# A four-layer graph network on one core: the second stage of edges ends behind node block 82 instead of 78

## The chip, the core and the metric

The kernel runs on one core of a Trainium2 chip. A core has a matrix engine (PE, with its weight loads shown apart as PEld), a vector engine (DVE), an activation engine (ACT), GpSimd (POOL), and a sync engine (SP) that only issues transfers. Each engine has its own instruction queue and works through it in order; they wait for each other by semaphores. Transfers move data between the large memory of the chip and the buffers beside the engines. The metric is the device time of one execution, in microseconds (us).

## The reference

A graph has 12,500 nodes with 32 features and 400,000 edges. `src` is random; `dst` is sorted, and low nodes have more edges than high ones (the share of the edges that goes to the first n nodes is the root of n/12500). Four layers follow each other. Each adds its result to x and normalises each row.

```python
edge_index = jnp.stack([src, dst])
x = _layernorm(x + _L0_gnn_ref(x, src, dst, ...))        # attention: softmax over the edges of a node
x = _layernorm(x + _L1_gnn_ref(x, edge_index, 3))        # three rounds: mean of the neighbours
x = _layernorm(x + _L2_gnn_ref(x, edge_index, edge_attr_32, ...))   # an MLP on each edge, maximum per node
x = _layernorm(x + _L3_gnn_ref(x, edge_index))           # three rounds: sum of the neighbours, scaled
...
# L2, on each edge
e_feat = jnp.concatenate([x[rol], x[col], edge_attr], axis=-1)
h = jax.nn.relu(e_feat @ W1 + b1)
v = h @ W2 + b2
x_cand = jax.ops.segment_max(v, col, num_segments=num_nodes)
return jnp.maximum(x_cand, x[:, -v.shape[-1]:])
# L3, one of three rounds
msgs = norm[:, None] * x[src]
x = jax.ops.segment_sum(msgs, dst, num_segments=n)
```

## The kernel before

Nodes are cut into H = 98 blocks of 128. A round of L1 or L3, a sum over the neighbours of every node, is done as a dense product: the kernel first builds the count matrix A (how many edges go from node s to node t, one byte each, 12,544 x 12,544, kept in the large memory), and then multiplies it with x. x stands in `x3` as three bf16 parts side by side (96 columns), so that nothing is lost.

`Rounds.product` is one such round. It takes the targets in 25 chunks c of 512 nodes (four blocks, the last chunk two) and, for each target block, one matmul per source block h: a 128 x 128 piece of A is the weight, the 96 columns of x3[h] stream past it (L382, 96 columns). It takes the source blocks from `lo` on; with lo = 0 that is 98 for each of 98 target blocks. Before the chunks comes a small extra product on `Ax`, for edges beyond what the build of A has room for in a chunk (c = -1, 392 matmuls of 128 columns, L377, then z at L310); its result is added to the first 14 chunks (L272). Loads of A go through SP (L354 where lo is above 0, two chunks of A in a buffer, L363 otherwise), into three buffers. Finished chunks are summed on DVE (L278).

The edge layer L2 (`edge_layer`) works on the edges themselves. A first part of them, 308 columns of 128 edges, is handled by `heavy` beside the rest. The other 2,817 columns are walked in stages. A stage s ends behind node block HS[s], and with the blocks a cut in the columns is fixed, with a margin of five deviations (`cuts`). A stage is cut into batches of up to T = 48 columns, and a batch into groups of four columns. For one group, POOL gathers four times the source rows from `table` (`ef<-table,ids`, L111), PE transposes them (pT, L1751), DVE copies (eT, L1753), PE and ACT run the MLP (`hidden`, L1782 to L1787, and `outer`, L1800). POOL may run up to AHEAD = 4 groups ahead, since a group's indices (`ids`, L1729) are copied behind an earlier group's eT. A batch also loads keep, attr and begin through SP (L1603, L1608, L1611), spreads the rows of the target nodes by 32 scans on DVE (L1628), takes running maxima by 32 more (L1637), and writes `scan` (L1640). At most two batches have an ef buffer; attr and begin have one.

The scans are emitted six to a group (`steps(6)`); those that a batch still lacks when it begins are emitted there at once.

When the last batch of a stage has its maxima, `end(s)` joins the partitions (a gather and a scatter, fx, on POOL), eight groups of delay among it, and `done(s)` gathers the maxima of the stage's node blocks from `scan` (`ends<-scan,end_i`, one gather for each block, in sets of G = 8), and finishes the layer on these blocks: layer norm, and x3 of L3's first round (`split`, its last step L258). `end` and `done` go on one step for each group (`tick`); behind the last stage they run through.

The stages are there for this: as soon as a stage's blocks have their x3, L3's first round can take their share while POOL still gathers edges. `round_part(s)` does that. It turns the product around: x3[h] is the weight (96 columns), and 512 targets of A stream past (L1366, 512 columns), for all 25 chunks and the blocks hs[s] to hs[s+1]. Each chunk's sum is copied (ys, L1373), turned by eight small matmuls (z, L284) and added to `part` (L1351). A chunk's blocks are loaded in pieces of up to HP = 16 blocks through SP (L1361), into three buffers. The steps are handed out by `fill`, called twice for a group, 40 steps on the first call of a part and eight on each later one; a step is one matmul. What is left when the edges are through is emitted behind the loop.

```python
hs = (0,) + HS + (H,)                       # L213
...
size = -(-(hi - lo) // -(-(hi - lo) // HP)) # L1342, in round_part
...
k = 8 if fillers[0] in begun else 40        # L1384, in fill
...
R.product(x3, post3, (), 0 if r else HS[-1])  # L1532: L3's rounds
```

So L3's first round consists of two parts of fill, blocks 0 to 51 and 52 to 77, and of a short product behind the edge layer, over the remaining 20 blocks (lo = HS[-1]). Memory for the product's buffers is taken over from the edge layer's.

The code gives the order only as a priority: a planner arranges each engine's queue at compile time from the order of the text, the dependences and its own costs, so an instruction may move ahead of an earlier one that it thinks is not ready. Tables for the edges (`edge_tables`) are prepared in pieces of at most 261 columns during L1.

With HS = (52, 78) the cuts are 308, 2292, 2804 and 3125: stages of 1984, 512 and 321 columns, in 42, 11 and 7 batches and 496, 128 and 81 groups. Stage 1's last batch has 32 columns.

Of the kernel before, what the change touches and what calls it, by code (L numbers as in the profile page):

```python
# [57 lines left out]

SPAN = 60.0
ONE = 512.0  # L60
HS = (52, 78)
EARLY = 2
CX = 14
HC = 308
# [56 lines left out]
def dense_path(ctx, tc, bad_i, x, src, dst, edge_attr, w1T, w1_b, w2, w2T, w2_b, aT,  # L121
# [90 lines left out]

    hs = (0,) + HS + (H,)  # L213
    cuts = [HC]
    for h in HS:
        f = (h * P / N) ** 0.5
        cuts.append(-(-int(E * f + 5 * (E * f * (1 - f)) ** 0.5) // P // 4) * 4)
    cuts.append(C)
    heads = []
    for s in range(len(HS) + 1):  # L220
        heads.append((
# [259 lines left out]
    def edge_tables(st):  # L481
# [25 lines left out]
        todo = []  # L507
        for s in range(len(HS) + 1):
            Cs = cuts[s + 1] - cuts[s]
# [166 lines left out]
    with ExitStack() as build:  # L676
# [164 lines left out]
        def slots():  # L841
# [31 lines left out]
            yield  # L873
            for s, h in enumerate(HS):
                w = slice(h % 4 * (P // W), h % 4 * (P // W) + 1)
# [313 lines left out]
    with ExitStack() as st:  # L1189
# [3 lines left out]
        with tc.tile_pool(name="seg", bufs=1) as seg, \  # L1193
# [18 lines left out]
            nc.vector.tensor_scalar(tot, tot, -1.0, 0.0, op0=OP.add, op1=OP.max)  # L1212
            for s in range(len(HS) + 1):
                sl = slice(hs[s], hs[s + 1])
# [1254 lines left out]
```

## Time and profile before

| what | us |
|---|---|
| median of 18 runs | 7686.87 (7679.53 to 7704.0) |
| the profiled execution | 7693.49 |
| its span, first to last instruction | 7691.6 |
| first matmul of the first fill, L1366 | at 5599.4 |
| last gather of an edge column | at 6549.2 |
| last matmul group of the second fill done | at 6594.2 |
| x3 of the last blocks written, short product goes on | at 6631 |
| first matmul of L3's second round | at 6751.9 |

The granted clock of PE was 0.832 on average. A page of the profile gives, for each engine, busy time in 40 slices of the span (tenths; 9 is 90% or more) and the granted clock likewise. A table by stage gives for chosen stretches the busy time of each engine with the number of instructions, then the granted clock, the share of time in which the transfer engines were busy, and GB/s. A line of the order of time gives the start, the length, the engine, the source line, the operation with the names of its output and inputs, and in brackets how long the engine was idle before it and what ended that. Where equal instructions follow each other closely they stand in one line with their number.

### The profile page before, as it was taken

The numbers are of one execution on the slowest core, as the hardware profiler recorded it, in microseconds if no ns is written. First come the engines' busy times: TensorE is split into PE (matmuls) and PEld (weight loads), VectorE is DVE, ScalarE is ACT, GpSimd is POOL, SyncE is SP. The second block draws the span as 40 slices with busy tenths as digits, with TensorE's granted clock in tenths as the row PEclk, the third lists the DMA queues.
The fourth block names the chain that finished last, engine by engine and source line by source line (L and its number), as shares of the span: only waits on it lengthen the run. The fifth ranks groups of instructions, "written<-read, shape, count | busy, mean of one in ns | idle before, by whom it ended". The sixth has DMA issues, their size and how long they took to land. (4 is left out here: it accounts for less than half of the span.)

```text
span 7691.6 us, 194318 instructions
## 1 busy us (share of the span) xinstructions
PE 6654.0 (87%) x84402; PEld 5288.6 (69%) x84402; DVE 3923.3 (51%) x10962; ACT 1635.5 (21%) x3386; POOL 3579.3 (47%) x3459
## 2 busy tenths in 40 slices
PE   6788999899999987888888888778669979899998
PEld 4678899889999984555555555434335645799998
DVE  6989899561554555555555555433344333411121
ACT  1334688200000002222222222211112212100000
POOL 1002501000655727777777777777777777100000
PEclk7879999999999996677777777555559968999999
DMA  2128544899999982222222222221227836799998
GB/s 51 65 109 323 196 202 198 301 334 361 361 373 354 362 323 78 62 55 55 59 55 63 55 55 59 51 60 46 52 74 225 250 87 185 247 352 366 356 355 311
DMA packets 574338, 1447.42 MB, mean 188 GB/s; under 512 B 108023, under 2 KB 269407, under 8 KB 560031
## 3 DMA queue, kind: packets, MB, share of 16 engines
q1 hardware_dynamic: 432816, 1347.10, 47.9%
q0 software_dynamic: 109792, 66.25, 5.1%
q10 hardware_dynamic: 30864, 21.54, 1.0%
q8 instruction: 664, 10.88, 0.6%
q14 instruction: 202, 1.65, 0.1%
HBM read 1155.33 MB, written 279.27 MB: 187 GB/s over the span
## 5 line engine op out<-in xcount | busy, mean ns | idle before, releaser
L111 POOL DMA_INDIRECT ef<-table,ids x2817 | 2677.0, 950 | 881.7 <-issue 654.5
L382 PE MATMUL y<-x,a 128*128 128x96 bf16 x49980 | 2217.1, 206 | 98.3 <-issue 97.3
L382 PEld LDWEIGHTS <-a 128*128 128x128 fp8e4 x49980 | 2156.0, 98 | 130.1 <-issue 128.0
L1751 PE MATMUL pT<-ident,ef 128*96 128x128 f32 x2817 | 770.8, 356 | 569.2 <-DMA ef<-table,ids 552.9
L1751 PEld LDWEIGHTS pT<-ident,ef 128*96 128x96 f32 x2817 | 398.5, 162 | 1026.3 <-DMA ef<-table,ids 681.5
L1753 DVE COPY eT<-pT 96x512 f32<-96x512 f32 x705 | 476.7, 676 | 1047.1 <-PE pT L1751 1046.6
L1019 PE MATMUL pa<-oh,ol 128*128 128x196 bf16 x4928 | 734.7, 273 | 121.2 <-DVE oh L1009 75.7
L1800 PEld LDWEIGHTS pv<-mw,hT 128*128 128x128 f32 x3208 | 598.1, 260 | 269.1 <-issue 94.0
L1025 ACT ACTIVATE at<-pa 128x784 uint16<-128x784 f32 x816 | 646.9, 824 | 506.2 <-PE pa L1019 477.5
L1800 PE MATMUL pv<-mw,hT 128*128 128x64 f32 x3208 | 679.5, 349 | 22.5 <-ACT hT L1787 15.2
L1787 ACT ACTIVATE hT<-ph,mb 128x256 f32<-128x256 f32 x802 | 380.5, 474 | 1332.2 <-PE ph L1784 1304.7
L1019 PEld LDWEIGHTS <-ol 128*128 128x128 bf16 x4928 | 558.9, 150 | 136.3 <-issue 74.8
L1055 PE MATMUL y<-x,at 128*128 128x102 bf16 x9604 | 641.6, 210 | 10.2 <-DVE x L258 6.0
L1782 PE MATMUL ph<-eT,mw 96*64 96x256 f32 x1410 | 627.1, 538 | 11.8 <-DVE eT L1753 10.3
L1784 PE MATMUL ph<-eT,mw 96*64 96x256 f32 x1408 | 629.4, 540 | 0.0
L278 DVE TENSOR_REDUCE v<-y 128x128 f32<-128x384 f32 (+2 forms) x152 | 83.4, 548 | 1067.3 <-PE y L272 582.0
L1009 DVE TENSOR_TENSOR oh<-bins_h,pl 128x1568 bf16<-128x1568 bf16 x616 | 594.6, 965 | 0.0
L111 POOL DMA_INDIRECT g<-code_d,ws_i x25 | 216.0, 8639 | 810.2 <-DVE ki L793 591.1
L116 POOL DMA_INDIRECT sorted_d<-hrow,pos x308 | 409.8, 1331 | 381.2 <-DVE v L1249 190.6
L1055 PEld LDWEIGHTS <-at 128*128 128x128 fp8e4 x9604 | 558.4, 98 | 23.6 <-issue 11.6
L1366 PE MATMUL y<-a,x 128*96 128x512 fp8e4 (+1 forms) x1950 | 492.4, 389 | 2.4 <-DVE x L258 1.5
L1004 DVE TENSOR_TENSOR ol<-la,lb 128x1024 bf16<-128x1024 bf16 x616 | 419.4, 683 | 69.5 <-PE pa L1019 69.1
(409 smaller groups left out, 6816.3 us busy)
## 6 DMA issues: line engine op xcount, KB each, us to landing
a<-A SPq DMA_DIRECT2D x245, 3136.0 KB
A<-at SPq DMA_DIRECT2D x98, 1568.0 KB
a<-A SPq DMA_DIRECT2D x144, 832.0 KB
ef<-table,ids POOLq DMA_INDIRECT x2817
starts_d<-rows SPq DMA_DIRECT2D x44, 1024.0 KB
attr<-in_edge_attr SPq DMA_DIRECT2D x57, 768.0 KB
begin<-starts_d SPq DMA_DIRECT2D x57, 768.0 KB
scan<-o SPq DMA_DIRECT2D x57, 768.0 KB
```

What stands on the lines that cost most here:

```text
L111: return nc.gpsimd.indirect_dma_start(out=o, out_offset=None, in_=tab, in_offset=IndirectOffsetOnAxis(ap=idx, axis=0))
L382: nc.tensor.matmul(y[:, q, :], block(h, q - q0), x3[:, h, :3 * F], start=(q + h == first), stop=(c >= CX and q == nq - 1 and h == H - 1))
L1009: nc.vector.tensor_tensor(oh, bins_h[:, None].to_broadcast([P, 4, HJ, 2]), pairs(pl[:, t, 0, half * 64 + w0:half * 64 + w0 + 8])[:, :, Non ...
L1019: nc.tensor.matmul(pa[:, 2 * b + i, :HJ], ols[t][:, :, :, 4 * u + 2 * b + i].rearrange("p a b -> p (a b)"), ohs[t][:, 2 * u + b, :, i], st ...
L1025: nc.scalar.activation(at[:, qd, :, off:off + 8].rearrange("p h (w j) -> p h w j", w=4), pa[:, :, :HJ].rearrange("p w (h j) -> p h w j", h ...
L1055: nc.tensor.matmul(y[0][:, q, :], at[:, q - 2 * half, h, :], x3[:, h, :3 * F0], start=(q + h == 0), stop=(not EARLY <= c < CX and last and ...
L1366: nc.tensor.matmul(y[:3 * D, :nq * Q], x3[:, h, :3 * D], a[:, :nq, h - h0, :], start=(h == lo), stop=(h == hi - 1))
L1751: nc.tensor.transpose(pT[:3 * D, j, :], B.ef[:, t + j, :], ident)
L1753: behind = nc.vector.tensor_copy(eT[:, :k], pT[:3 * D, :k])
L1782: nc.tensor.matmul(ph[:HID, :ka], mw1, eT[:, :ka], start=True, stop=True)
L1784: nc.tensor.matmul(ph[HID:2 * HID, :k - 2], mw1, eT[:, 2:k], start=True, stop=True)
L1800: nc.tensor.matmul(pv[:, j].rearrange("p h d -> p (h d)"), hT[:, j, :], mw2, start=True, stop=True)
```

## The change

One constant is changed. The second stage ends behind block 82. The cuts become 308, 2292, 2872 and 3125: stages of 1984, 580 and 253 columns, in 42, 13 and 6 batches and 496, 145 and 64 groups; stage 1's last batch has four columns, a single group. The second part of the fill has 30 blocks (52 to 81) in two pieces of 15 instead of two of 13, `done(1)` has 30 blocks and `done(2)` 16, and the short product starts at lo = 82, with 16 source blocks. Edge tables are prepared in 12 pieces as before, three of up to 194 columns for stage 1 and one of 253 for stage 2 (before: two of 256, and 161 and 160).

```diff
@@ -58,7 +58,7 @@
 
 SPAN = 60.0
 ONE = 512.0
-HS = (52, 78)
+HS = (52, 82)
 EARLY = 2
 CX = 14
 HC = 308
```

## The prediction

> **What bounds the kernel now.** I first read the page's slices of the span, to find which engine is full where. Slices are 192 us long, so the edge layer's end (6100 to 6600 us) is slices 32 to 35.
>
> ```profile
> PE   6788999899999987888888888778669979899998
> POOL 1002501000655727777777777777777777100000
> PEclk7879999999999996677777777555559968999999
> ```
>
> POOL is level at 7 through the edge layer, while PE and its clock go up and down. The table by stage, with stages cut where the second fill starts and ends, says why.
>
> ```profile
> core 0: us, PE busy (x) PEld busy (x) DVE busy (x) ACT busy (x) POOL busy (x), PEclk, DMA share, GB/s
> 6195.00:6395.00 200.00, 140.99 (x452) 68.93 (x452) 76.91 (x298) 32.40 (x85) 151.55 (x160) 0.56 0.23 59
> 6395.00:6570.00 175.00, 175.00 (x1038) 111.45 (x1037) 60.13 (x230) 35.75 (x85) 110.03 (x117) 1.00 0.71 216
> 6594.00:6631.00 37.00, 9.39 (x96) 8.73 (x95) 14.42 (x49) 2.84 (x9) 19.21 (x20) 0.62 0.69 254
> 6651.00:6740.00 89.00, 87.20 (x1989) 86.08 (x1987) 53.62 (x167) 13.11 (x44) 0.00 (x0) 1.00 0.84 305
> ```
>
> From 6195 to 6395 there is nothing to fill with; POOL starts a gather every 1.25 us (160 in 200 us) and sets the pace. From 6395 PE is full: edges and fill compete, and POOL falls behind its pace. From 6594 to 6631 PE has 9 us of work in 37. Then the short product is PE's. The same table for the fill's matmuls alone (L1366) gives their number:
>
> ```profile
> core 0: us, PE busy (x) PEld busy (x), PEclk, DMA share, GB/s
> 6395.00:6570.00 175.00, 121.91 (x503) 58.65 (x504) 1.00 0.71 216
> 6570.00:6595.00 25.00, 18.54 (x92) 10.37 (x90) 1.00 0.56 164
> ```
>
> The order of time shows the seam (start, length, work, and the idle time before it with its cause):
>
> ```profile
> 6383.00 1.09 PE L1366 MATMUL y<-a,x 128*96 128x512 fp8e4 x2 [0.17 <-DVE x L258]
> ...
> 6549.18 0.95 POOL L111 DMA_INDIRECT ef<-table,ids  x1 [0.34 <-DVE ids L1729]
> 6570.25 0.27 PE L1751 MATMUL pT<-ident,ef 128*96 128x128 f32 x1
> 6577.89 7.09 PE L1366 MATMUL y<-a,x 128*96 128x512 fp8e4 x32
> 6588.28 0.95 POOL L111 DMA_INDIRECT fx<-scan,fix  x1 [38.16 <-DMA a<-A]
> 6593.53 0.63 PE L284 MATMUL z<-S,ys 96*128 96x32 f32 x4 [0.51 <-ACT ys L1373]
> 6604.39 5.83 PE L377 MATMUL y<-a,x 128*96 128x128 fp8e4 x56 [10.22 <-issue]
> 6618.10 0.94 POOL L111 DMA_INDIRECT ends<-scan,end_i  x1 [0.30 <-issue]
> 6717.78 21.93 PE L382 MATMUL y<-x,a 128*128 128x96 bf16 x512 [0.33 <-issue]
> 6751.87 23.68 PE L377 MATMUL y<-a,x 128*96 128x128 fp8e4 x392 [3.26 <-DMA a<-Ax]
> ```
>
> The second fill starts as the last x3 block of stage 1 is written (6383), the last edge column is transposed at 6570, the fill ends at 6594.2, and the gathers of the last 20 node blocks end at 6619. Only when their x3 is written (6631) does the short product go on. So fill and edges end almost together, and the tail of `done(2)` is what PE waits for.
>
> **The change, part by part.**
>
> *Where the second fill starts.* Groups of four columns are the clock of the emission. Stages have 496, 128 and 81 groups before and 496, 145 and 64 after. Counting yields: `end(1)` begins 14 groups after stage 1's end (17 after the change, because its last batch is one group long), `done(1)` another 14 later, and `round_part(1)` is appended 19 later (21 with 30 blocks). That is group 671 of 705 before, 693 after. The first call takes 40 steps, each later one 8, two calls a group: 40+8+33·16 = 576 of 25·26 = 650 matmuls are emitted inside the loop before; 40+8+11·16 = 224 of 25·30 = 750 after. Left behind the loop: 74 before, 526 after. The trace fits the first count: 92 matmuls from 6570 on, 74 plus one group's 16.
>
> *Time of that start.* The 22 groups in between are paced by POOL: 22·4 gathers and 4 more end gathers in `done(1)`, at 1.25 us, 115 us. PE becomes full at 6395+115 = 6510. Lower bound 100 (three groups of the count are scan pacing that could shrink), upper 135 (below, the short batch).
>
> *The full stretch.* Before it lasts 6395 to 6594.2, 199.2 us. Taken out: 22 groups of edge work. In the 175 us row, 503 fill matmuls at 0.216 (32 in 7.09 us, less the last one's tail) are 108.6 us and 160 z matmuls (20 chunks at 0.82) 16.4; the other 50 us are 31 groups, 1.6 each: -35.2. Put in: 100 matmuls at 0.216, +21.6. So 185.6 us, and the fill ends at 6695.6. Check from the other side: the last transposes come some 8 us earlier than before, at 6562, since POOL is less held back; 542 matmuls, 18 z and the edges' rest of 4.5 us follow, 117+15+4.5, giving 6698.
>
> *Loads of the fill on SP.* Still 50 issues, but 15 blocks each instead of 13, 6.5 MB more. A chunk of 1.97 MB is used up in 30·0.216+0.82 = 7.3 us, 270 GB/s. The trace sustained 246 GB/s from 5800 to 6180 beside edge traffic and 305 in the short product, so I take no wait; at 246 it would be 0.7 us for each of 17.5 chunks, +12, and at the 216 GB/s of the row above 1.8, +32. Queued behind these loads on SP is only the last `scan` write, and the x3 that hangs on it has some 70 us to spare.
>
> *The tail of stage 2.* 16 gathers, not 20: -5 us on POOL, and one `finish` less. It now ends near 6615, under the fill, so it costs and gains nothing. If the fill were short again it would be worth 5 us.
>
> *The short product (lo 82).* 98·4 = 392 matmuls of 96 columns fewer, at 0.0425 (512 in 21.93): -16.7 us. Its loads fall by the same 6.5 MB; they are hidden by PE before (87 of 89 us) and stay so. Between the fill's end and the next round's first matmul lie 157.7 us before (6594.2 to 6751.9). After: 10.2 waiting for `Ax` (no longer hidden, but there already), 392 L377 at 60 to 66 ns, 25; 97.8 (6650.8 to 6748.6) less 16.7, 81.1; the next `Ax` wait, 3.3, grows by 1.7 since the last two and a half chunks cover less of a load: 5. Sum 121.3, a gain of 36.4. Of this, some 20 us are simply the PE wait that the longer fill has moved into.
>
> *One batch more.* 61 instead of 60: two keeps, attr, begin and a scan write on SP, and 64 scans of 0.2 to 0.3 us on DVE, which is busy 77 of 200 us: free. But stage 1's last batch is a single group, so 26 of the next batch's 32 scans are forced at its start, and its gathers must wait for the PE to finish the batch before the short one. No row has this; the same place before has 8 forced scans and no POOL gap. From nothing to 20 us; I take 0, as POOL runs several groups ahead and PE has 59 us of slack in that stretch. Preparation of the edge tables keeps 12 chunks and every element: nothing.
>
> *Sum.* 6695.6 - 6594.2 - 36.4 = +65 us. On the profiled execution, 7693.49 (span 7691.6), that is 7758; it stood 6.6 above the median, so for the median 7686.87 I forecast 7752.
>
> **A page against the trace.** PE streams 216 ns for each 512-column matmul in the row of 32 and 42.5 ns for each 96-column one in the row of 512. The Trainium skill, "TensorE: Matmul & The Clock Gate", section "Back-to-back issue gap", gives about 131 ns at 512 columns and 81 at 128 for a stream of weight loads and matmuls. By the page the 100 added matmuls would cost 13 us and the 392 removed save 32, an estimate of +41 instead of +65: it speaks for the change, and the rows contradict it.
>
> **The rivals.**
>
> Faster: the planner draws the fill forward so that it still ends under the tail. PE has 59 idle us from 6195 to 6395 (clock 0.56), which speaks for it; but x3 blocks 52 up exist only when `done(1)` has written them, and before the change the fill started within a microsecond of the last. The point is a fill's end of 6631: 65 us, 300 matmuls, would have to find room earlier. If all did, the time falls by 16.7+5-1.7 = 20, to 7667.
>
> Same: half of that room is found, or the 22 groups shrink to about 10; the fill ends within 15 us of 6631. Near 7687.
>
> Slower still: the long pure fill outruns its three load buffers, +12 to +32, so 7764 to 7784. If its waits also let the clock drop to the 0.5 of the unfilled stretches, 526 matmuls at twice 0.216 add 114: 7866.
>
> That the change does nothing is excluded: cuts, groups and blocks all move.
>
> **How the numbers follow.** As worked 0.73 (own range 7735 to 7775, from the bounds on the start, -15 and +20); loads bind 0.15; clock drops 0.03; same 0.05; faster 0.04. Changes of 0.2%, 15 us, are about what a measurement tells here. Slower 0.91, same 0.05, faster 0.04. The range 7718 to 7788 holds the first two cases and leaves out about 0.12 and their edges.
>
> **What would show it.** Right: the fill's matmuls run without edge transposes beside them for over 100 us, ending near 6695; the last end gather lies well before; PE is full from about 6510; the short product has 1568 L382 matmuls in some 81 us; the rest keeps its lengths. Wrong: fill matmuls starting before 6480, their pitch off 0.216, gaps in them released by DMA, or POOL idle at the third stage's start.

## The result and the profile after

The changed kernel takes 7768.23 us (median of 7 runs, 7758.21 to 7782.81) against 7687.17 for the kernel before beside it: a ratio of 1.0105, with a 95% interval from 1.0095 to 1.0115. It is 81 us slower; 65 were forecast, a time of 7752. The profiled execution of it took 7764.42, with a span of 7762.6.

The slices of the page, in order PE, POOL and the granted clock of PE:

```profile
PE   6788999999999988888888888678679978899998
...
POOL 1003401001566637777777777777777775000000
PEclk7889999999999986776777777555579958999999
```

POOL's row is as level as before. Slices of 194 us are too coarse for the rest: where the edge layer ends, slice 33 has a tenth of the clock less (5 instead of 6) and slice 34 a tenth of PE (8 instead of 9). The table by stage, cut where the same stages now lie:

```profile
core 0: us, PE busy (x) PEld busy (x) DVE busy (x) ACT busy (x) POOL busy (x), PEclk, DMA share, GB/s
6179.00:6380.00 201.00, 145.02 (x448) 70.44 (x449) 84.42 (x363) 34.82 (x87) 152.14 (x161) 0.51 0.24 62
6495.00:6549.00 54.00, 52.11 (x301) 32.14 (x300) 21.52 (x88) 9.84 (x24) 31.62 (x34) 1.00 0.73 221
6549.00:6703.00 154.00, 136.72 (x712) 86.19 (x710) 24.13 (x94) 14.52 (x31) 17.37 (x18) 0.93 0.70 219
6736.00:6818.00 82.00, 79.41 (x1811) 78.67 (x1808) 55.23 (x176) 13.71 (x46) 0.00 (x0) 1.00 0.82 290
```

The stretch with edges alone is still paced by POOL (161 gathers in 201 us), PE and edges compete for only 54 us where it was 175, and then comes what was hardly there before: 154 us in which the edges are through and PE works on the fill. In that row the clock is 0.93 and PE is busy for 136.72 of 154 us. The order of time on PE shows where the rest is (start, length, work, and the idle time before it with its cause):

```profile
6548.93 0.27 PE L1751 MATMUL pT<-ident,ef 128*96 128x128 f32 x1
...
6577.18 6.66 PE L1366 MATMUL y<-a,x 128*96 128x512 fp8e4 x30
6584.48 6.65 PE L1366 MATMUL y<-a,x 128*96 128x512 fp8e4 x30
...
6607.44 1.91 PE L284 MATMUL z<-S,ys 96*128 96x32 f32 x8 [16.31 <-ACT ys L1373]
...
6609.17 9.28 PE L1366 MATMUL y<-a,x 128*96 128x512 fp8e4 x30
...
6619.10 6.66 PE L1366 MATMUL y<-a,x 128*96 128x512 fp8e4 x30
...
6702.12 0.63 PE L284 MATMUL z<-S,ys 96*128 96x32 f32 x4 [0.51 <-ACT ys L1373]
```

A chunk of the pure fill takes 7.3 us, 30 matmuls between two z in 6.66 us and the z, from the last transposes at 6549 to the end at 6702.75. But once PE stands for 16.31 us, because z waits for the copy `ys`, and the 30 matmuls behind the hole run at a lower clock, 9.28 us instead of 6.66. ACT's own order says why the copy is late:

```profile
6582.41 0.58 ACT L1373 COPY ys<-y 96x512 f32<-96x512 f32 x1 [6.72 <-PE y L1366]
6603.54 0.21 ACT L243 ACTIVATE ln_s<-ln_s 128x8 f32<-128x8 f32 x1 [20.55 <-DVE ln_s L242]
...
6606.50 0.41 ACT L257 CAST x<-rest 128x256 bf16<-128x256 f32 x1 [0.72 <-DVE rest L256]
6606.81 0.57 ACT L1373 COPY ys<-y 96x512 f32<-96x512 f32 x1
```

L243 belongs to the layer norm of `done(2)`, and L254 and L257 behind it to the writing of x3. L243 waits for DVE, and DVE waits twice for the end gathers of the last 16 blocks, which come in two sets of eight:

```profile
6595.58 0.42 DVE L1309 TENSOR_TENSOR ends<-ends,rest 128x256 f32<-128x256 f32 x1 [17.92 <-DMA ends<-scan,end_i]
...
6603.00 0.42 DVE L1309 TENSOR_TENSOR ends<-ends,rest 128x256 f32<-128x256 f32 x1 [2.98 <-DMA ends<-scan,end_i]
```

The chunk that is to be copied was through at about 6589.7 (24 of the 30 matmuls of the line at 6584.48 belong to it, the last six to the next one; the copy before, at 6582.41, came at the same point of the line at 6577.18). But the copy stands behind L243, L254 and L257 in ACT's queue, and runs 17 us late. Loads are not the cause: no wait of PE in these 154 us is for one, and SP's queue waits for PE to free the buffers (total, times, longest):

```profile
SPq L1361 <- PE y L1366: 122.1, 33, 22.6
```

To hold the two executions against each other I count from the last edge gather of the first stage, which the change doesn't touch (5377.2 before, 5365.8 after). The 11 us between these two are no more than lies between two executions of one kernel: the changed kernel's second trace, on another chip (below), has 5352.0.

| term | before | after | difference | forecast |
|---|---|---|---|---|
| that gather to PE full with the second fill (its 60th matmul) | 1019.4 | 1129.6 | +110.2 | +115 |
| PE full to the fill's end | 197.6 | 207.3 | +9.7 | -13.6 |
| fill's end to L3's second round | 157.7 | 120.1 | -37.6 | -36.4 |
| sum | 1374.7 | 1457.0 | +82.3 | +65 |

From the second round to the end both take 939.7 or 939.8 us. The sum is 17 us over the forecast; the second term alone is 23 over it, and the other two take 6 back.

### The profile page after: what moved, and what is told of

The parts are those of the page before. It is cut to its first block, busy times and chain, and to the rows that moved or that the text cites. A ratio compares the mean times of both kernels' runs of the same rounds, so it can differ in the third digit from the quotient of the medians.

```text
span 7762.6 us, 193783 instructions
## 1 busy us (share of the span) xinstructions
PE 6694.0 (86%) x84110; PEld 5293.6 (68%) x84110; DVE 3925.4 (51%) x11010; ACT 1635.0 (21%) x3385; POOL 3577.1 (46%) x3459
## 5 line engine op out<-in xcount | busy, mean ns | idle before, releaser
L1751 PE MATMUL pT<-ident,ef 128*96 128x128 f32 x2817 | 790.9, 360 | 599.3 <-DMA ef<-table,ids 580.5
L1366 PE MATMUL y<-a,x 128*96 128x512 fp8e4 (+1 forms) x2050 | 508.9, 389 | 1.1 <-DMA a<-A 0.7
```

The costliest lines, as they stand in the source:

```text
L1366: nc.tensor.matmul(y[:3 * D, :nq * Q], x3[:, h, :3 * D], a[:, :nq, h - h0, :], start=(h == lo), stop=(h == hi - 1))
L1751: nc.tensor.transpose(pT[:3 * D, j, :], B.ef[:, t + j, :], ident)
```

## Experiments

My theory was the forecast's with the hole added: the fill starts some 110 us late because the work that releases it goes by groups from a later stage end, what then lies behind the edge loop goes at PE's pace, the short product gives some 37 back, and ACT's queue adds some 20. The rivals: that the four more source blocks cost, with their loads; that the hole is harmless; that the one-group batch stalls the gathers; and that fewer blocks are better all along.

The chips differ. The first four runs were on one that takes 9021.67 us for the kernel before (median of 14 runs); the others were on chips that take 7676.01 (21 runs) and 7687.95 (19 runs). Each run is held against the kernel before on its own chip.

### The two halves of the change

The cut of the edges and the list of blocks come from the same constant; here they are given apart.

```diff
+CUTS = (52, 82)        # edges only: HS stays (52, 78); blocks only: the two exchanged
-    for h in HS:
+    for h in CUTS:
         f = (h * P / N) ** 0.5
...
-            for s, h in enumerate(HS):
+            for s, h in enumerate(CUTS):
```

> Half of the change alone: the edges of stage 2 are cut where the change cuts them (for node block 82), but only blocks up to 78 are made out of that stage, and the fill and the product behind the edge layer stay as before (12 chunk rows of the fill, 20 source blocks behind it). Theory (the fill is made after the stage's last gathers, which the longer stage puts 15 to 20 groups of 6 us later, and what then lies behind the edge loop runs at TensorE's pace; the scalar queue's stalled layer norm adds one hole of about 16 us with a slow chunk behind it, if it falls into the fill): fill start +95 us, fill shorter from full issue to its end by some 32 us, so the fill ends 62 us later, or 82 with the hole; the product behind it has 20 blocks, but its gathered rows wait less, which gives some 20 back. Against before: +42 us without the hole, +62 with it. Rival (the four more source blocks of the fill, their loads and matmuls, are what costs): within 15 us of before.

> The other half: the edge stages stay cut for node block 78, but blocks up to 82 are made out of stage 2 and go into the fill, and 16 source blocks are left behind it. (It leaves out: the maxima of blocks 79 to 81 are gathered before their last edges are through, so a few of their edges don't count.) Theory (late start of the fill): the fill starts within 15 us of before, has 50 more matmuls per pass behind the loop, ends some 34 us later, and the short product gives 36 back: -3 to +17 us against before, the upper end if the hole on TensorE is still there. Rival (more blocks in the fill and their loads are the cost): most of the 81 us, +50 or more.

> The edges' cut for block 82 with the blocks of 78, again, on another chip. Theory (the later end of the stage costs, not the four more blocks): fill start some 100 us later than before, some 410 matmuls behind the loop, the hole of the scalar queue in it, the product with 20 blocks: +50 to +65 us against before. Rival (the blocks cost): within 15 us of before.

Edges alone: 1.0082 (1.0054 to 1.0110), +74 us on the slow chip, 12 more than expected there, and 1.0074 (1.0057 to 1.0091), +56.5 us, on the other, as expected. There the fill's first matmul comes 97 us later than before and its 60th 101, counted from the first stage's last gather, with 410 matmuls behind the last transposes. Blocks alone, in a kernel that leaves out a few edges: 1.0017 (1.0001 to 1.0033), +16 us. So the later stage end is what costs, and the four blocks nearly pay for themselves. The hole is there in the cut-only run too. On the faster chip the profile puts it down to a step of the same layer norm on DVE; but the copy that z reads ended on ACT at 6617.61, 0.05 us before z began, and it stood there directly behind the same L243, L254 and L257 (one line further down in this kernel). PE's line, then ACT's:

```profile
6617.66 1.92 PE L285 MATMUL z<-S,ys 96*128 96x32 f32 x8 [20.17 <-DVE ln_s L238]
```

```profile
6617.03 0.58 ACT L1374 COPY ys<-y 96x512 f32<-96x512 f32 x1
```

With blocks alone a wait of 17.4 us for `ys` was left behind the last transposes.

### The hole in ACT's queue

The layer norms of the last blocks are put behind the fill:

```diff
+            if s == len(HS):
+                while fillers:
+                    fill(0)
+                with tc.issue_after(last[0].ins), tc.issue_after(last[1].ins):
+                    for t in todo:
+                        for _ in finish(*t):
+                            pass
+                return
```

(`last` holds the latest `ys` copy and the latest addition to `part`.)

> The changed kernel, with the last blocks' layer norm and x (the tail of stage 2) put on the scalar and vector queues behind the last copy and the last addition of the fill, so that no copy of the fill stands behind a wait for the end gathers. Theory (the scalar queue's order makes the 16 us hole and the slow chunk behind it): no wait of TensorE over 2 us within the fill, the fill ends some 20 us earlier, and the time is 15 to 20 us under the changed kernel's, +61 to +66 us against before; if the tail then ends too late for the next layer, up to 10 of that are lost again at the first product. Rival (the hole is covered, or TensorE waits for something else there): within 4 us of the changed kernel, +77 to +85.

> The changed kernel itself, on the chip of the runs beside it, so that these can be held against it. +81 us against before on a chip that takes 7687 us for before; on a chip that is slowed to some 9022 us, where a group of the edge loop takes 7.9 us in place of 6.2, the fill's start is moved by 20 to 22 such groups and the change costs more, +95 to +115 us.

> The same kernel as e3_tail_order, now beside the changed kernel on the same chip. Theory (the scalar queue's order makes the hole, and the hole costs its length): 15 to 20 us under the changed kernel. Rival (the slow granted clock would have come anyway, or the delayed tail of stage 2 takes the gain back at the next layer's first product): within 5 us of the changed kernel, although the hole is gone.

The first of these runs showed no wait of PE over 2 us behind the last transposes (ahead of them, beside the edges, one of 10.5 us for `ys`), but the changed kernel wasn't beside it, so its 1.0100 (1.0072 to 1.0128), +93 us on the slow chip, tells nothing of the hole's price. Beside each other on a third chip: the changed kernel 7752.25 us, 1.0102 (1.0083 to 1.0120), +76 us; with the tail behind the fill 7739.17, 1.0079 (1.0063 to 1.0096), +63 us. The medians differ by 13, under the 15 to 20 expected, and the intervals overlap. The two profiled executions as wholes are no help either, 7746.41 and 7746.98: the reordered one comes 15.3 us later to the last gather of the first stage, long before the part that the edit concerns, which is as much as between two executions of one kernel. The traces of the stretch itself are sharper. The fill from the last transposes to its end, in the changed kernel and then in the reordered one:

```profile
core 0: us, PE busy (x) PEld busy (x) DVE busy (x) ACT busy (x) POOL busy (x), PEclk, DMA share, GB/s
6536.00:6690.00 154.00, 136.31 (x712) 85.96 (x709) 24.23 (x94) 14.52 (x31) 17.29 (x18) 0.93 0.69 219
```

```profile
6553.00:6687.00 134.00, 132.93 (x712) 84.43 (x709) 13.23 (x62) 12.56 (x25) 17.05 (x18) 1.00 0.78 251
```

The same 712 instructions take 134 us instead of 154, at a clock of 1.00 and 251 GB/s. The waits of PE in these two stretches:

```profile
PE z L284 <- ACT ys L1373: 16.7, 2, 16.2
```

```profile
PE z L284 <- ACT ys L1383: 0.5, 1, 0.5
```

From the last transposes to the fill's end it is 153.3 against 133.8 us, 19.5 less: 16.2 are the hole, 3.3 the slow chunk behind it. Nothing of it is lost later, since from the fill's end to the second round it is 120.0 in both. Counted as in the table, the reordered kernel's terms are +111.0, -8.6 and -37.7: +64.7. So that the wait on ACT's queue makes the hole is shown; its price is 19.5 us in the traces and 13 in the medians.

### An earlier start of the fill

Even batches in the second stage (g groups of four columns in nb batches, in place of full batches and a rest of one group):

```diff
+            g, t0 = -(-Cs // 4), 0
+            for j in range(nb):
+                n = min(4 * (g // nb + (j < g % nb)), Cs - t0)
+                plan.append((s, t0, n))
+                t0 += n
```

> The changed kernel, with the 332 column tiles of stage 2 in batches of nearly even size in place of full ones and a last batch of one group. Theory (the fill's start is counted in groups from the end of the stage, and the three groups' time of a short batch goes through the count): the fill is made at group 687 in place of 693, starts some 35 us earlier, and the time is 25 to 30 us under the changed kernel's, about +50 against before. Rival 1 (the short batch itself stalls the gather queue): a gap goes from GpSimd and TensorE at the start of stage 3, and more than 30 us are saved. Rival 2 (the batches' size is without effect): +77 to +85 us against before.

This gave 1.0059 (1.0036 to 1.0081), +55 us, on the slow chip: 37 us under the reordered kernel, the only one with the changed cuts and blocks beside it, although the hole is still there (15.9 us). 446 matmuls are left behind the last transposes instead of 542, exactly six groups of 16 fewer, so the count holds. The fill's first matmul comes 51 us earlier than in that run; 38 of them lie behind the end of the second stage, six groups of 6.3 us, and 13 ahead of it, which the count doesn't explain, so on this chip the first rival isn't excluded. On the changed kernel's own chip there is next to nothing of it: POOL stands for 3.22 us behind the one-group batch, where it stood 1.77 at the same place before (6099.14), and then goes on as before, 161 gathers in 201 us:

```profile
6179.08 0.95 POOL L111 DMA_INDIRECT ef<-table,ids  x1 [3.22 <-ACT part L1353]
```

Then the waiting work is taken twice per group in the third stage:

```diff
-            steps(6)
-            tick()
+            for _ in range(2 if B.s == 2 else 1):
+                steps(6)
+                tick()
```

> The changed kernel, with the steps of the waiting work taken twice per edge group in the groups of stage 3, so that the end gathers of stage 2, which release the fill, come after half as many groups. Theory (the fill's late start is the cost): the fill is made at group 667 in place of 693, starts within 15 us of where it does before, ends some 80 to 95 us earlier than in the changed kernel, and the time is -18 to +5 us against before (up to +15 with the hole on TensorE). Rival 1 (the start was not what cost; four more blocks are): +60 to +80 against before. Rival 2 (the edge loop pays for the work that is pushed into fewer groups): the last gather of the edge layer comes more than 15 us later, and +20 to +50.

> Both together: twice the steps per group in stage 3, and the tail of stage 2 behind the fill on the scalar and vector queues. Theory: fill at group 667, no hole on TensorE, -20 to 0 us against before, 0 to 20 under the run with twice the steps alone. Rival (the tail of stage 2, delayed behind the fill, ends last): 5 to 20 us over the run with twice the steps alone.

With the steps doubled, block 82 takes 7672.80 us, 0.9993 (0.9982 to 1.0004): all of the 76 us are gone, and the edit changes only how soon the waiting work, the scans with it, is taken. The fill's first matmul comes 74 us earlier than in the changed kernel (21 later than before; I had said within 15) and its 60th 126 us earlier (17 earlier than before), 126 matmuls are left behind the last transposes instead of 542, and the fill ends 108 us earlier (80 to 95 were expected), 20 of them the hole, which is gone because the end gathers now come back after the fill. The last edge gather comes 8 us later than in the changed kernel, under the 15 of the second rival.

Both edits together: 7661.92 us, 0.9979 (0.9970 to 0.9988), 14 us or 0.2% under the kernel before and the fastest kernel of this study on its chip. But the reorder has no part in that which the trace shows: there was no hole left for it to remove. With the steps doubled alone as with both, PE's waits for `ys` in the fill are one of 0.5 us. In both traces the second round starts 1365 us after the first stage's last gather. The 11 us between their medians are unexplained, and their intervals overlap.

### The neighbours: 80, 74, and an earlier fill at 78

```diff
-HS = (52, 78)
+HS = (52, 80)        # and (52, 74); the third keeps 78 and takes the steps twice
```

> Half of the step: stage 2 ends behind node block 80, so 18 source blocks are left for the product. Theory (the fill's late start against the wait for the tail of stage 2, some 20 us, that the longer fill first has to use up): the fill is made at group 683 in place of 671 (before) and 693 (block 82), starts 60 to 65 us later than before, leaves some 320 matmuls behind the loop, and the time is +25 to +45 us against before. Rival (the cost is in proportion to the blocks added, as that of a loop with four more blocks would be): just half of the change's +76 to +81, and no more wait left at 78 blocks to be used up, so that 74 blocks would gain another 76.

> The same step the other way: stage 2 ends behind node block 74, 24 source blocks are left. Theory (before the change the product waits for the tail of stage 2, not for the fill): the fill is over before the last edges, the first product matmul of the next layer that has to wait for the tail comes within 5 us of where it comes before, and the product is 4 blocks, some 15 us, longer: +10 to +20 us against before. Rival (fewer blocks are better all along): -40 to -80.

> The kernel before, with the steps of the waiting work taken twice per edge group in stage 3: the fill comes earlier, at group 648 in place of 671. Theory (before the change the fill's end isn't what the product waits for): the fill ends inside the edge loop, the tail of stage 2 and all behind it stay, within 8 us of before, and so over the run with block 82 and twice the steps by the four blocks of the product, 10 to 15 us less what that run's fill still costs. Rival (an earlier fill is a gain by itself, whatever the blocks): -15 us or more against before.

Block 80: 7723.23 us, 1.0045 (1.0028 to 1.0061), +35 us, as expected, with 332 matmuls behind the last transposes and a hole of 15.7 us; the fill's first matmul comes 47 us later than before and its 60th 57, a little under the 60 to 65 expected. Block 74: 7682.53 us, 0.9991 (0.9981 to 1.0001), -5 us, no gain or a small one where I expected a loss of 10 to 20. So the times stand at about -5, 0, +35 and +76 to +81 for 74, 78, 80 and 82: flat on one side of the kernel before and steep on the other. No proportion fits that.

What I missed at 74 is not the product. From PE's last wait for a block of the tail (it ends at 6604.00 at 74 and at 6631.18 before) to the second round it takes 134.2 us instead of 120.7: +13.5, near the 15 forecast. But that wait ends 17 us earlier, counted from the first stage's last gather, where I had said within 5. First POOL's order of time, then PE's, at 74:

```profile
6530.44 0.95 POOL L111 DMA_INDIRECT ef<-table,ids  x1 [0.30 <-issue]
6549.96 0.94 POOL L111 DMA_INDIRECT fx<-scan,fix  x1 [18.57 <-DMA scan<-o]
```

```profile
6600.27 1.09 PE L377 MATMUL y<-a,x 128*96 128x128 fp8e4 x8 [10.34 <-DVE x L258]
...
6604.00 6.19 PE L377 MATMUL y<-a,x 128*96 128x128 fp8e4 x72 [1.36 <-DVE x L258]
```

From the last edge gather to the join `fx` it is 19.5 us here and was 39.1 before (6549.18 to 6588.28), where the last groups' transposes and MLP stood among fill matmuls on PE: the last transpose came 21 us after the last gather before, and comes 4 us after it here. So the fill that ran until 6594 before was not free: beside the last edges it delayed the tail that PE then waited for. The run with 78 and doubled steps says the same: its fill is over 68 us before the last gather is issued, and `fx` comes 19.1 us after that gather. In POOL's order of time:

```profile
6554.17 0.94 POOL L111 DMA_INDIRECT ef<-table,ids  x1 [0.30 <-issue]
6573.26 0.94 POOL L111 DMA_INDIRECT fx<-scan,fix  x1 [18.14 <-issue]
```

Of these 20 us only some 5 are left where PE's last wait for the tail ends, since the last edge gather itself comes 9.5 us later than before and the tail behind `fx` takes longer. The run takes 7676.92 us, 0.9984 (0.9974 to 0.9993), -11 us; I had expected no more than 8 either way, and the rival 15 or more. It is on a par with block 82 and doubled steps (0.9993 and 0.9979 on their chip): once the fill is early enough, four blocks more or less in it are not to be told apart. What the shorter product saves at 82, 11.8 us by the same count (106.4 against the 118.2 of this run), the later tail takes back.

## Why the prediction was right, and where it was off

*Where the second fill starts.* The count was right to the matmul: 526 steps behind the loop and one group's 16 were forecast, 542 matmuls follow the last transposes. The even batches, with 96 fewer, confirm it. The time read from the trace was not the start: at 6383 only the last of four sets of x3 blocks was written, and from 6299.9 on, behind the first set, 59 matmuls of the fill had trickled through. So "nothing to fill with" until 6395 and a start "within a microsecond of the last" block were misread, and the sign "fill matmuls starting before 6480" came true without meaning anything: after the change the first is at 6384.9, and again 59 come before PE is full at 6495.5.

*Time of that start.* +115 forecast, +110 measured to the 60th matmul, where PE is full. That it is the cause was shown by the doubled steps, which take this delay away (and with it the hole) and leave cuts and blocks as they are, and by the two halves.

*The full stretch.* This is the mis-sized term: -13.6 forecast, +9.7 measured. Some 19 of the 23 us are the hole and the slow chunk behind it; with these removed the term is -8.6. The 5 us that remain cancel with the 4 of its start and the 1 of its product: the reordered kernel's sum is +64.7 against the +65 of the working. Its other parts held: 6.66 us for 30 matmuls (216 ns each, with the last one's tail), and the last transposes 10 us earlier (forecast: some 8).

*Loads of the fill on SP.* Right, no wait of PE for a load; without the hole the loads went at 251 GB/s.

*The tail of stage 2.* This is the step that failed: "ends near 6615, under the fill, so it costs and gains nothing". It named as cover the fill's length and the 70 us that its x3 has to spare. Both were there: the end gathers were back by 6603, and the last x3 was written at 6612.5. Yet it cost 19.5 us. But the tail's layer norm and the fill's copies share ACT and DVE, and each queue is worked through in order, so a wait that nobody needed to end soon stopped a copy that PE needed at once. The change adds no wait, so I didn't ask who is queued behind one; but an old wait had moved among new neighbours: before, the same layer norm came behind the fill's last copies. The Trainium skill, "TensorE: Matmul & The Clock Gate", section "Architectural detail: the array is 16× 32×32, not 1× 128×128", calls ACT's and DVE's queues strictly first in, first out; the copy at 6606.81, whose input was ready at about 6589.7, agrees.

*The short product.* -36.4 forecast, -37.6 measured, and right in its parts. The runs at 74 and with doubled steps put the four blocks at 11.8 to 13.5 us, where the working had 16.7; the rest was, as the working said, PE's former wait for the tail.

*One batch more.* Nearly nothing, as taken: POOL's wait behind the batch is 1.5 us longer than before. Its three groups were in the count of the start.

*The rivals.* The planner did not draw the fill forward. Loads did not bind. The clock did drop, but for one chunk: 2.62 us on its 30 matmuls and 0.93 on the z before them (1.91 instead of 0.98). Together these are 3.55 us. The same page, section "What's actually happening", has the clock at half after at least one idle window of some 3.4 us and back to full after at least one busy one; with one busy window the hole would have cost 1.7 us behind it, with two 3.4, both estimates, and the rows agree with two.

*The range.* 7768 lies in it, but partly by luck: the room above 7752 was given to a later start and to loads that bind, and neither came.

## What to carry to other kernels

A piece of work that is moved into a stretch shares every engine's queue with what was already there: besides what it costs and what covers it, ask for each in-order queue which of the waiting instructions now stand ahead of work that the bound engine needs. When the start of filling work is counted in steps of another loop, a later release costs one for one what no longer fits beside that loop; releasing it sooner (here, two steps per group) took back all of it, where even batches took back a part. And before a tuned size is moved, look which side of it is flat: in these runs, filling work that ended with the work it fills delayed that by some 20 us, while filling work that ended later added all of what was left of it.

## What was not expected of the hardware

One chip ran its kernels some 17% slower (9021.67 against 7676.01 us for the kernel before). In the same stretch of time, inside the first stage of the edge layer, the blocks-only kernel there and then the kernel before where it was profiled:

```profile
core 0: us, PE busy (x) PEld busy (x) DVE busy (x) ACT busy (x) POOL busy (x), PEclk, DMA share, GB/s
3600.00:5200.00 1600.00, 1174.23 (x5315) 723.16 (x5315) 657.83 (x2592) 314.29 (x816) 900.28 (x953) 0.60 0.17 43
```

```profile
3600.00:5200.00 1600.00, 1296.77 (x6434) 783.56 (x6433) 815.78 (x3230) 390.13 (x1011) 1211.33 (x1276) 0.67 0.24 57
```

POOL does 953 gathers in 1600 us instead of 1276, each as long as elsewhere (0.945 us against 0.949), at a granted clock of 0.60 instead of 0.67. POOL's waits there include one that the other trace hardly shows (5.5 us in 18 waits):

```profile
POOL ef L112 <- DVE ids L1730: 358.6, 103, 5.9
```

So on that chip the edge loop is no longer paced by POOL's own issue. The lower clock alone doesn't explain it. Where the first fill runs beside the edges the clock is high on both; the reordered kernel on the slow chip, then on the third one:

```profile
7300.00:7400.00 100.00, 89.88 (x486) 52.83 (x487) 33.23 (x143) 16.21 (x47) 58.45 (x62) 0.97 0.65 201
```

```profile
6000.00:6100.00 100.00, 100.00 (x576) 61.71 (x574) 39.78 (x159) 20.62 (x52) 71.64 (x76) 1.00 0.79 245
```

At 0.97 of the clock POOL still does 62 gathers in 100 us there, against 76. Some 280 of its lost 1371 us lie ahead of the edge layer, whose first gather is at 3163.3 against 2882.6, and from L3's second round to the end almost nothing is lost, 940.8 against 938.5 us. What slows the edge loop stays open. The cut alone costs on both chips, +74 and +56.5 us.
